# Layer 1's q product with a second Strassen step in four of its seven products

## The chip, the cores and the metric

The kernel runs on one core of a Trainium2 chip. The core has a matrix engine (TensorE: PE in the profile, PEld for its weight loads), a vector engine (DVE), a scalar engine (ACT), a general engine (POOL) and a queue engine (SP) that starts most transfers between HBM and the on-chip memory SBUF. PE writes its results to a second on-chip memory, PSUM, from which DVE and ACT take them. Every engine works through its own list of instructions in order, and waits for others through semaphores. The metric is the time of one execution in microseconds (us) on the device.

## The reference

Eight samples x of 512 channels by 1024 positions (32 x 32) go through two attention blocks, all in fp32. What matters here is the second one:

```python
def _L1_conv_ref(x, gn_gamma, gn_beta, wq, bq, wk, bk, wv, bv, wo, bo):
    mean = jnp.mean(x, axis=(1, 2, 3), keepdims=True)
    var = jnp.var(x, axis=(1, 2, 3), keepdims=True)
    n = (x - mean) * jax.lax.rsqrt(var + EPS)
    n = n * gn_gamma[None, :, None, None] + gn_beta[None, :, None, None]
    nf = n.reshape(b, c, h * w)
    q = jnp.einsum('oc,bcs->bos', wq, nf) + bq[None, :, None]
    k = jnp.einsum('oc,bcs->bos', wk, nf) + bk[None, :, None]
    v = jnp.einsum('oc,bcs->bos', wv, nf) + bv[None, :, None]
    attn = jax.nn.softmax(jnp.einsum('bci,bcj->bij', q, k) * c ** (-0.5), axis=-1)
    out = jnp.einsum('oc,bcs->bos', wo, jnp.einsum('bcj,bij->bci', v, attn)) + bo[None, :, None]
    return x + out.reshape(b, c, h, w)
```

The first block is a normalisation over groups of 16 channels, attention with eight heads of 64 channels, a projection, and `x + projection`. Its result is the x above.

## The kernel before

**Matrix products.** A product of 512 x 512 weights with 512 channels x 1024 positions is done by Strassen's method in Winograd's form: weights and data are cut into 2 x 2 quarters (`A11`.. and `B11`..), the sums `S1`..`S4` and `T1`..`T4` of them are formed, and seven products of quarters take the place of eight. A quarter of the data is `[128, 2, 512]`: two chunks k of 128 channels, 512 positions. A quarter product therefore takes two matmuls of 128 x 128 weights by 512 columns for each of two output chunks c. An fp32 matmul of the program is two PE instructions in the profile.

Products that run "twice" (q and k of layer 0, V of layer 1) apply the method a second time to four of the seven products, `PAIRS`: each of those four is again seven products, of 128 x 128 weights by half the columns. The three that remain are called lines (`A11 B11`, `S2 T2`, `S3 T3`) and add up in one PSUM bank for each output chunk. The quarter sums that the second step needs are made by `sums_a` from the weights (stored in HBM once, reloaded by `WeightTwice`) and by `quarters_b` from the data: three DVE instructions for each of `B21`, `T1`, `B22`, `T4`.

**Layer 1's weights.** Since q and k meet only in q'k, one matrix wqk1 takes the place of both; "q" is wqk1' x, and x itself stands for k. In the same way wvo1 is V and the output projection in one. Normalisation is not applied to x: `norm.c` is a bias of q worked out from mean and deviation, and `norm.factor` goes into the exponential.

**Order.** The program is unrolled over the eight samples, and the order on PE, DVE and ACT is the order in which the code is written (`manual_schedule`). A product is a Python generator that yields after each of its steps; `together` lets several take turns, and `at_steps` runs hooks after step n. What a hook issues stands in its engine's list at that place, so an early instruction that waits holds up all that stands behind it on its engine.

The stages of one sample that matter here, with the names of the code:

- `pairs_qk_twice` (layer 0, of the next sample): steps 0 to 13 are the second-step products of L862, steps 14 to 19 the lines of L869, added by DVE on L585. At hook 18 and 19 `divide_at` (L980) divides the attention's result by its sums, and `combine2` (L1030) makes T1 to T4 of the projection's data.
- `project` (PE on L632 into `ps_p`): `together(project(w, 0), project(w, 1))`, ten steps. ACT copies partial results (L425), DVE adds (L1229), adds the residual (L1215, x is complete there) and takes statistics of every chunk and half of x with `norm.of_half` (`bn_stats`, L318); `norm.of_channels` (`bn_aggr`, L321) brings them together at the end.
- `attention1`, `make_q` (PE on L632 into `ps_q`): the seven products of q, ten steps. At its hooks DVE makes T1 to T4 (`combine.make`, L400), the mean and deviation of the sample (`mean_of_all`, `deviation`: two small matmuls on L299 stand among q's), and the quarter sums for V (`halve_b`: L494 and L500). ACT finishes q with scale gamma and bias `norm.c` (L1291).
- `make_v_twice` (PE on L890 and L647): V's product, with the quarter sums of `halve_b`.
- scores, exponentials, values and the output follow.

At the start of the program the merged weights are made (`product`, `product_in_quarters`), their rows scaled by gamma on ACT (`scale_rows`, L235), the sums `S1`..`S4` formed (`finish`, L194) and the second-step sums made and stored (`WeightTwice(..., make)`, L477).

## Time and profile before

| | us |
|---|---|
| median of 3 runs | 2834.16 (2832.84 to 2834.77) |
| the profiled execution, its own time | 2834.0 |
| its span, from first to last instruction | 2832.3 |
| PE busy in the span | 2815.8 (mean granted TensorE clock 0.999) |
| sample 1: `project` on PE | 593.02 to 618.39: 25.37, DVE busy 17.81, ACT 3.51 |
| sample 1: q on PE | 618.39 to 642.87: 24.48, DVE busy 18.88, ACT 8.61 |
| longest wait of PE shown anywhere | 2.0 (before V's lines in the last sample) |

In the timeline a row is a run of equal instructions: its start in us from the start of the span, how long it took, the engine, the line, what is written and read, the shape, and how many there were; in brackets the idle time of that engine before it and what ended it. The start of a PE row is when it really began; its end is modelled, since matmuls are pipelined, so the distance from start to start is what counts. The same holds on DVE and ACT, where the next instruction starts some 0.1 us before the last one is written, unless it needs its result.

### The profile page before, as it was taken

Reading aid. Unit: us, or ns where it says so; the run is one execution under the profiler, and the core shown is the slowest. Engines: PE = TensorE matmul, PEld = TensorE weight load, DVE = VectorE, ACT = ScalarE, POOL = GpSimd, SP = SyncE. Lnnn points to the kernel's source line nnn. Section 1 sums busy time; section 2 is a strip of 40 time slices with the busy share of each in tenths; the row PEclk is TensorE's granted clock in tenths of the full one; section 3 lists DMA queues with packets and bytes.
Section 4 is the critical chain, followed back from the end, with each engine's and each line's share of the span. In section 5 each row is a group of like instructions: output and inputs, shape, how many; then the busy total and the mean of one; then the engine's idle time right before and its main releaser. Section 6 shows DMA issues by size and latency. Waiting matters only on the chain.

```text
span 2832.3 us, 38612 instructions
## 1 busy us (share of the span) xinstructions
PE 2815.8 (99%) x15496; PEld 1549.6 (55%) x15496; DVE 2124.0 (75%) x2979; ACT 1101.2 (39%) x1536; POOL 273.6 (10%) x236
## 2 busy tenths in 40 slices
PE   9999999999999999999999999999999999999999
PEld 5434765347643476444773456734567346673365
DVE  6677696767867778776777777777777777767877
ACT  3462324623256232552325522265232642326432
POOL 0000220003100040000400004000040000400011
PEclk9999999999999999999999999999999999999999
DMA  8422131321323213133131331313213142121001
GB/s 290 164 76 86 54 125 64 87 89 53 112 68 91 83 68 104 59 91 108 56 108 45 88 108 56 108 49 96 96 59 105 49 119 72 64 88 55 8 16 39
DMA packets 81123, 237.75 MB, mean 84 GB/s; under 512 B 21512, under 2 KB 22312, under 8 KB 74536
## 3 DMA queue, kind: packets, MB, share of 16 engines
q1 hardware_dynamic: 74456, 212.11, 23.1%
q10 hardware_dynamic: 6480, 23.10, 2.4%
q8 instruction: 124, 2.03, 0.3%
q14 instruction: 63, 0.52, 0.1%
HBM read 179.37 MB, written 31.98 MB: 75 GB/s over the span
## 4 chain that ended last, share of the span: by engine, by line
PE 89%; DVE 7%; DMA 2%; issue 1%; SPq 0%; ACT 0%; POOL 0%; DVEq 0%; POOLq 0%
PE s L941 16%; PE ps_o L960 15%; PE ps_q L632 8%; PE ps_v L647 7%; PE ps_o L1535 7%; PE ps_p L632 5%; PE ps_l L1371 4%; PE ps_s L1354 4%; PE ps_s_qk L862 4%; PE ps_l_qk L869 3%; PE ps_l_v L647 3%; PE ps_s L1371 3%; PE ps_o_qk L862 3%; PE ps_s_v L890 2%; PE ps_s_two L1665 2%; PE ps_o_v L890 1%
## 5 line engine op out<-in xcount | busy, mean ns | idle before, releaser
L798 ACT ACTIVATE p<-s 128x1024 f32<-128x1024 f32 x512 | 523.7, 1025 | 329.0 <-PE s L941 322.2
L800 DVE TENSOR_TENSOR acc<-acc,p 128x1024 f32<-128x1024 f32 x384 | 469.9, 1224 | 100.9 <-ACT p L798 92.5
L960 PE MATMUL ps_o<-p,v 64*64 64x512 f32 x4096 | 528.6, 589 | 0.0
L941 PE MATMUL s<-c_q,c_k 64*64 64x512 f32 x3584 | 465.1, 590 | 0.0
L960 PEld LDWEIGHTS ps_o<-p,v 64*64 64x64 f32 x4096 | 156.6, 133 | 282.9 <-issue 278.0
L941 PEld LDWEIGHTS s<-c_q,c_k 64*64 64x64 f32 x3584 | 134.7, 133 | 253.2 <-issue 236.1
L339 POOL TENSOR_TENSOR rstd<-rstd,minus_half 128x4 f32<-128x4 f32 (+1 forms) x16 | 19.8, 1239 | 2081.8 <-DVE rstd L338 2081.8
L1535 PE MATMUL ps_o<-t_p,s_v 128*128 128x512 f32 x384 | 168.2, 594 | 0.0
L800 DVE TENSOR_TENSOR acc<-p,p 128x1024 f32<-128x1024 f32 x64 | 78.3, 1224 | 80.0 <-ACT p L798 80.0
L1345 ACT ACTIVATE p<-p,factor 128x512 f32<-128x512 f32 (+1 forms) x112 | 85.3, 780 | 115.7 <-DVE p L1381 90.9
L1535 PEld LDWEIGHTS ps_o<-t_p,s_v 128*128 128x128 f32 x384 | 72.3, 190 | 91.3 <-issue 89.2
L1359 ACT COPY p<-ps_s 128x512 f32<-128x512 f32 x96 | 53.1, 588 | 177.0 <-PE ps_s L1354 177.0
L632 PE MATMUL ps_p<-t_p,w_p 128*128 128x512 f32 x256 | 115.2, 598 | 5.9 <-DVE u_p L1229 4.6
L1381 DVE TENSOR_TENSOR p<-ps_l,p 128x512 f32<-128x512 f32 x136 | 90.1, 684 | 40.5 <-PE ps_l L1371 40.2
L632 PE MATMUL ps_q<-t,w_wqk 128*128 128x512 f32 x256 | 116.1, 598 | 0.0
L425 ACT COPY u_v<-ps_v 128x512 f32<-128x512 f32 x48 | 28.1, 586 | 204.9 <-PE ps_v L647 195.8
L1381 DVE TENSOR_TENSOR p<-ps_s,p 128x512 f32<-128x512 f32 x112 | 74.9, 685 | 37.9 <-PE ps_s L1371 37.9
L647 PE MATMUL ps_v<-w_v,t_again 128*128 128x256 f32 x448 | 99.0, 379 | 0.0
L425 ACT COPY u_p<-ps_p 128x512 f32<-128x512 f32 x48 | 28.1, 585 | 174.1 <-PE ps_p L632 174.1
L425 ACT COPY u_q<-ps_q 128x512 f32<-128x512 f32 x54 | 31.2, 578 | 160.7 <-PE ps_q L632 160.7
L647 PEld LDWEIGHTS ps_v<-w_v,t_again 128*128 128x128 f32 x448 | 85.1, 190 | 11.6
L632 PEld LDWEIGHTS ps_p<-t_p,w_p 128*128 128x128 f32 x256 | 47.4, 190 | 72.4 <-issue 53.6
(463 smaller groups left out, 4948.2 us busy)
## 6 DMA issues: line engine op xcount, KB each, us to landing
x<-in_x SPq DMA_DIRECT2D x92, 512.0 KB, 6.5
w_qk<-stored_qk SPq DMA_DIRECT2D x14, 1792.0 KB, 7.1
w_wqk<-stored_wqk SPq DMA_DIRECT2D x8, 1792.0 KB, 7.6
fold<-acc SPq DMA_DIRECT2D x56, 256.0 KB, 3.1
inv<-inv_rows SPq DMA_DIRECT2D x56, 256.0 KB, 5.0
qk_twice<-stored_qk_twice ACTq DMA_DIRECT2D x28, 512.0 KB, 6.3
w_wvo<-stored_wvo SPq DMA_DIRECT2D x8, 1792.0 KB, 7.5
out<-x SPq DMA_DIRECT2D x28, 512.0 KB, 4.7
```

What stands on the lines that cost most here:

```text
L425: nc.scalar.copy(us[n][:, :width], line[:, :width])
L632: nc.tensor.matmul(bank, w[a][:, k, c * P : (c + 1) * P], bs[b][:, k, :], start=fresh and k == 0, stop=k == 1, skip_group_check=True,)
L647: nc.tensor.matmul(bank[:, u * 2 * P : (u + 1) * 2 * P], bs[b][:, k, n * P : (n + 1) * P], w[a][:, k, :], start=fresh and u == k == 0, sto ...
L798: nc.scalar.activation(p, s, AF.Exp, scale=factor)
L800: nc.vector.tensor_tensor(acc, first, p, ALU.add)
L862: nc.tensor.matmul(bank[:, i * 2 * P : (i + 1) * 2 * P], parts[a][x], twice_b[v][y], start=start and i == 0, stop=True, skip_group_check=True,
L941: nc.tensor.matmul(s[cols, j, :], ks[pair][k0 // HALF][rows, k0 % HALF : k0 % HALF + HD], qs[pair][g][rows, :], start=True, stop=True,)
L960: nc.tensor.matmul(o[cols, half, :], vs[kt][rows, c0 : c0 + HD], p[rows, j, :], start=kt == 0, stop=kt == NT - 1,)
L1354: nc.tensor.matmul(bank, bs[v][:, k, t * P : (t + 1) * P], q_parts[a][:, k, :], start=a == "A11" and k == 0, stop=k == 1, skip_group_check ...
L1371: nc.tensor.matmul(bank[:, u * 2 * P : (u + 1) * 2 * P], v[y][:, u * P : (u + 1) * P], a[x], start=start and u == 0, stop=True, skip_group ...
L1381: nc.vector.tensor_tensor(at(r, t), bank, at(r, t), ALU.add)
L1535: nc.tensor.matmul(bank, v_parts[kt // 2][a][:, kt % 2, c * P : (c + 1) * P], p_parts[kt // 2][b][:, kt % 2, cols], start=fresh and kt == ...
```

## The change

- q's product now runs "twice" as V's does, with its own order of pairs, `PAIRS_Q`. One generator makes both output chunks: two second-step products (f for `A12 B21` and `S4 B22`, s for `S1 T1` and `A22 T4`) around the lines. Its second-step weights are reloaded for each sample (`WeightTwice("wqk1")`: two transfers of 512 KB on ACT's queue), and made and stored once at the start.
- The quarter sums of x serve q and V. Those of `B21` and `B22` move into the stage before, `project`.
- Gamma of q's output channels is multiplied into the weights at the start (`scale_both`, on DVE, with a row of gamma loaded by one more transfer), so q needs only a bias at its end.
- The statistics of half of x are taken by ACT: for each chunk one half is taken by DVE (`first_half`), the other by two ACT instructions with accumulators (`second_half`), brought together by six small DVE instructions (`both_halves`).
- `combine2` of the projection's T2 to T4 moves from the hook ahead of `project` into its steps, and the four divisions change places.

```diff
+        def first_half(self, cc, half):
+            part = self.part[:, cc, 0, :]
+            nc.vector.bn_stats(part, piece(self.xs, cc, half))
+            nc.vector.bn_aggr(self.stat[:, :, cc], part)
+
+        def second_half(self, cc, half):
+            x = piece(self.xs, cc, half)
+            to = onepool.tile([P, HALF], FP, tag="held", name=f"from_0_{self.name}_{cc}")
+            nc.scalar.activation(to, x, AF.Identity, accum_out=self.part[:, cc, 1, 0:1])
+            to = onepool.tile([P, HALF], FP, tag="held", name=f"from_mean_{self.name}_{cc}")
+            nc.scalar.activation(
+                to, x, AF.Square, bias=self.stat[:, 0, cc : cc + 1], scale=-1.0,
+                accum_out=self.part[:, cc, 1, 1:2],
+            )
...
+    PAIRS_Q = [[("A12", "B21"), ("S4", "B22")], [("S1", "T1"), ("A22", "T4")]]
...
-                18: [lambda pair=pair: divide_at(pair, 0) for pair in couple],
-                19: [lambda pair=pair: divide_at(pair, 1) for pair in couple]
-                + [lambda n=n: combine2(n, 1) for n in range(1, 5)],
+                18: [lambda g=g: divide_at(couple[0], g) for g in range(2)],
+                19: [
+                    lambda: divide_at(couple[1], 0), lambda: combine2(1, 1),
+                    lambda: divide_at(couple[1], 1),
+                ],
...
-                    norm.of_half(chunk, half)
+                    if i == half:
+                        norm.first_half(chunk, half)
+                    else:
+                        norm.second_half(chunk, half)
+                    if (i, half, c) == (1, 0, 1):
+                        ready.halve("B21")
...
-        at_steps(together(project(w, 0), project(w, 1)), {})
-        for cc in range(NC):
-            norm.of_channels(cc)
+        hooks = {} if last else {2 * n - 3: [lambda n=n: combine2(n, 1)] for n in range(2, 5)}
+        hooks[0] = [ready.load]
+        hooks[7] = [lambda: ready.halve("B22")]
+        at_steps(together(project(w, 0), project(w, 1)), hooks)
...
+        def make_q(w):
...
+                for bank, x, y, start, use, r, t in [
+                    (line, "A11", "B11", True, nc.scalar.copy, 0, 0),
+                    (single, "A12", "B21", True, add, 0, 0),
+                    (line, "S2", "T2", False, nc.scalar.copy, 0, 1),
+                    (single, "S1", "T1", True, nc.scalar.copy, 1, 1),
+                    (line, "S3", "T3", False, add, 1, 1),
+                    (single, "S4", "B22", False, add, 0, 1),
+                    (line, "A22", "T4", False, nc.scalar.copy, 1, 0),
+                ]:
...
+            def take(r):
+                c11 = first[r][:, 0, :]
+                nc.vector.tensor_tensor(c11, lines[r], c11, ALU.add)
+
+            quarters = pair(PAIRS_Q[0], first, "f")
+            for n in range(2):
+                next(quarters)
+                yield
+            for r in range(2):
+                multiply(r, "A11", "B11", True)
+                yield
+            for n in range(5):
+                next(quarters)
+                if n == 0:
+                    take(0)
+                if n == 4:
+                    take(1)
+                yield
+            for r in range(2):
+                multiply(r, "S2", "T2", False)
+                c12 = first[r][:, 1, :]
+                nc.vector.tensor_tensor(c12, lines[r], c12, ALU.add)
+                yield
+            yield from pair(PAIRS_Q[1], second, "s")
+            for r in range(2):
+                nc.scalar.activation(
+                    piece(qs, r, 0), first[r][:, 0, :], AF.Identity, bias=norm.c[:, r : r + 1]
+                )
+                final(r, 0, 1, second[r][:, 0, :], first[r][:, 1, :])
+            for r in range(2):
+                multiply(r, "S3", "T3", False)
+                for n, half in enumerate([1, 0]):
+                    final(r, 1, half, lines[r], second[r][:, n, :])
+                yield
...
+        def statistics():
+            norm.both_halves()
+            norm.mean_of_all()
+
+        at_steps(make_q(w), {
+            1: [lambda: combine.make(1)],
+            6: [lambda: combine.make(2)],
+            8: [lambda: twice_w.append(WeightTwice("wvo1"))],
+            9: [lambda: combine.make(4)],
+            10: [lambda: ready.halve("T1"), lambda: ready.halve("T4")],
+            12: [statistics],
+            13: [lambda: combine.make(3)],
+            14: [norm.deviation],
+            16: [norm.untaken],
         })
...
-            wqk1.scale_rows(V_NW1)
+            wqk1.scale_both(V_NW1, gamma_row)
...
+                lambda: WeightTwice("qk02", both_of(w)), lambda: WeightTwice("wqk1", columns_of(wqk1)),
```

`final` is one DVE instruction (`x + norm.c + y`); `add` and `take` are one each; `nc.scalar.copy` is ACT. In `attention1` the old `make_q` and its hooks are removed.

More of the change, by code (lines that the diff above doesn't have):

```diff
@@ L79, in two_attention_blocks @@
     vectors: bass.AP,
+    gamma1: bass.AP,
     out: bass.AP,
@@ L235, in scale_rows, with scale_both @@
                     nc.scalar.activation(a, a, AF.Identity, scale=vec[:, by + cc : by + cc + 1])
+        def scale_both(self, by, row):
+            for cc in range(NC):
+                for to, a in self.moving(cc):
+                    nc.vector.scalar_tensor_tensor(
+                        a, a, vec[:, by + cc : by + cc + 1], row[:, to], ALU.mult, ALU.mult
+                    )
         def finish(self):
@@ L323, in of_channels, with both_halves @@
             )
+        def first_half(self, cc, half):
[11 more added lines that the diff above has]
+            )
+        def both_halves(self):
+            mean, var = self.stat[:, 0, :], self.stat[:, 1, :]
+            d, q = self.part[:, :, 1, 0], self.part[:, :, 1, 1]
+            nc.vector.scalar_tensor_tensor(d, d, 1.0 / HALF, mean, ALU.mult, ALU.subtract)
+            nc.vector.scalar_tensor_tensor(mean, d, 0.5, mean, ALU.mult, ALU.add)
+            nc.vector.scalar_tensor_tensor(q, q, 1.0 / HALF, var, ALU.mult, ALU.add)
+            nc.vector.scalar_tensor_tensor(d, d, -0.5, d, ALU.mult, ALU.mult)
+            nc.vector.tensor_tensor(var, q, d, ALU.add)
+            nc.vector.tensor_scalar(var, var, 0.5, None, ALU.mult)
         def mean_of_all(self):
@@ L1205, in layer0 @@
         bias = made["bias0"]
-        later = []
+        later, ready = [], Ready(xs, b)
         def project(w, c):
@@ L1247, in layer0, with __init__, load, halve @@
         w = next_weight().parts[0]
-        at_steps(together(project(w, 0), project(w, 1)), {})
-        for cc in range(NC):
-            norm.of_channels(cc)
+        hooks = {} if last else {2 * n - 3: [lambda n=n: combine2(n, 1)] for n in range(2, 5)}
+        hooks[0] = [ready.load]
+        hooks[7] = [lambda: ready.halve("B22")]
+        at_steps(together(project(w, 0), project(w, 1)), hooks)
         if last:
             held(invs.pop(end), f"inv_0_{b}_{end}_1")
-        return xs, norm, qs_next, ks_next
-    def attention1(xs, norm, b, at_values):
+        return xs, norm, ready, qs_next, ks_next
+    class Ready:
+        def __init__(self, xs, b):
+            self.combine, self.quarters, self.b = Combined(f"1_{b}"), {}, b
+            self.combine.take(xs)
+        def load(self):
+            self.weights = WeightTwice("wqk1")
+        def halve(self, name):
+            self.quarters[name] = quarters_b(
+                self.combine.parts[name], tile2(f"{name}_twice_{self.b}")
+            )
+    def attention1(xs, norm, ready, b, at_values):
         last = b + 1 == B
@@ L1266, in attention1 @@
         qs = quarters_of(f"q_1_{b}")
-        w = next_weight().parts[0]
+        w = next_weight()
         twice_w = []
-        combine, later = Combined(f"1_{b}"), []
-        combine.take(xs)
+        combine = ready.combine
         bs = combine.parts
-        twice_a, twice_b = {}, {}
+        twice_a, twice_b = {}, ready.quarters
         def halve_a(name, t=None, engine=nc.vector):
@@ L1278, in halve_a @@
             twice_a[name] = sums_a(q, flat(tile2(f"{name}_twice_{b}")) if t is None else t, engine)
-        def halve_b(name):
-            twice_b[name] = quarters_b(bs[name], tile2(f"{name}_twice_{b}"))
-        def make_q(c):
-            def done(i, half, bank, u):
-                n, to = c + 2 * i, piece(qs, c + 2 * i, half)
-                if u is not None:
-                    nc.vector.tensor_tensor(u, bank, u, ALU.add)
-                    bank = u
-                def scaled():
-                    nc.scalar.activation(
-                        to, bank, AF.Identity, bias=norm.c[:, n : n + 1],
-                        scale=vec[:, V_NW1 + n : V_NW1 + n + 1],
-                    )
-                if i == half == 0:
-                    later.append(scaled)
-                else:
-                    scaled()
-            return strassen(by_channels(w, c, bs), done, f"q_1_{b}_{c}")
@@ L1303, in attention1, with pair, add, multiply @@
-        at_steps(together(make_q(0), make_q(1)), {
-            0: [lambda: combine.make(1)],
-            1: [lambda: combine.make(2)],
-            2: [norm.mean_of_all, lambda: combine.make(3)],
-            3: [lambda: halve_b("B21")],
-            4: [norm.deviation, lambda: combine.make(4)],
-            6: [lambda: halve_b("T1")],
-            7: [lambda: halve_b("B22")],
-            8: [lambda: halve_b("T4")],
-            5: [lambda: twice_w.append(WeightTwice("wvo1")), norm.untaken, lambda: later.pop(0)(), lambda: later.pop(0)()],
+        def make_q(w):
+            parts = ready.weights.all(columns_of(w))
+            first, second = ([tile2(f"{n}_q_1_{b}_{r}") for r in range(2)] for n in ["c11", "c22"])
+            lines = [banks("o", f"ps_l{r}_q_1_{b}") for r in range(2)]
+            spares[:] = [line[:, 1, :] for line in lines]
+            lines = [line[:, 0, :] for line in lines]
+            def pair(products, to, name):
+                line, single = (banks("s", f"ps_{name}{n}_q_1_{b}")[:, 0, :] for n in range(2))
+                def add(at, bank):
+                    nc.vector.tensor_tensor(at, bank, at, ALU.add)
+                for bank, x, y, start, use, r, t in [
[7 more added lines that the diff above has]
+                ]:
+                    for i, (a, v) in enumerate(products):
+                        nc.tensor.matmul(
+                            bank[:, i * 2 * P : (i + 1) * 2 * P], parts[a][x], twice_b[v][y],
+                            start=start and i == 0, stop=True, skip_group_check=True,
+                        )
+                    use(
+                        to[r][:, :, t * 2 * P : (t + 1) * 2 * P],
+                        bank.rearrange("p (i q) -> p i q", i=2),
+                    )
+                    yield
+            def multiply(r, a, v, fresh):
+                by_channels(w.parts[0], r, bs)(lines[r], a, v, fresh)
+            def final(r, i, half, x, y):
+                n = r + 2 * i
+                nc.vector.scalar_tensor_tensor(
+                    piece(qs, n, half), x, norm.c[:, n : n + 1], y, ALU.add, ALU.add
+                )
+            def take(r):
[24 more added lines that the diff above has]
+                    piece(qs, r, 0), first[r][:, 0, :], AF.Identity, bias=norm.c[:, r : r + 1]
+                )
+                final(r, 0, 1, second[r][:, 0, :], first[r][:, 1, :])
[3 more added lines that the diff above has]
+                    final(r, 1, half, lines[r], second[r][:, n, :])
+                yield
+            spares.clear()
@@ L1724, in two_attention_blocks @@
         norm = norm0(xs_next, 0)
+        gamma_row = tile2("gamma_row")[:, 0, :]
+        nc.sync.dma_start(gamma_row, gamma1.to_broadcast([P, C]))
         class Through(Rows):
@@ L1778, in two_attention_blocks @@
             4: [lambda: combine.make(4)], 5: [lambda: WeightTwice("wvo1", columns_of(wvo1))],
-            7: [wqk1.finish], 8: [waiting[0].finish], 9: [lambda: WeightTwice("qk02", both_of(w))],
+            7: [wqk1.finish], 8: [waiting[0].finish], 9: [
+                lambda: WeightTwice("qk02", both_of(w)), lambda: WeightTwice("wqk1", columns_of(wqk1)),
+            ],
         })
@@ L1786, in two_attention_blocks @@
                 ahead = [norm0(load_x(b + 1, nc.sync), b + 1)]
-            xs, norm, qs, ks = layer0(bs, qs, ks, b, ahead[0] if b + 1 < B else None)
+            xs, norm, ready, qs, ks = layer0(bs, qs, ks, b, ahead[0] if b + 1 < B else None)
             at_values = {}
@@ L1802, in two_attention_blocks @@
                 bs = combine_next.parts
-            attention1(xs, norm, b, at_values)
+            attention1(xs, norm, ready, b, at_values)
 @with_exitstack
@@ L2180 @@
         "n_v1": np.ascontiguousarray(inputs["L1_conv_wv"]),
+        "gamma1": np.ascontiguousarray(np.asarray(inputs["L1_conv_gn_gamma"]).reshape(1, C)),
     }
```

## The prediction

> **What bounds the kernel now.** I read the page first: PE is busy for 99% of the span and makes 89% of the chain that ended last, so what counts is how many matmul columns PE streams and where it stands still.

> ```profile
> PE 2815.8 (99%) x15496; PEld 1549.6 (55%) x15496; DVE 2124.0 (75%) x2979; ACT 1101.2 (39%) x1536; POOL 273.6 (10%) x236
> PE 89%; DVE 7%; DMA 2%; issue 1%; SPq 0%; ACT 0%; POOL 0%; DVEq 0%; POOLq 0%
> ```

> Then PE's timeline in sample 1 (the others repeat it):

> ```profile
> 569.76 0.59 PE L862 MATMUL ps_s_qk<-t,w_qk 128*128 128x256 f32 x2
> 570.20 0.59 PE L862 MATMUL ps_s_qk<-x,w_qk 128*128 128x256 f32 x2
> ...
> 593.02 7.03 PE L632 MATMUL ps_p<-o,w_p 128*128 128x512 f32 x16
> 600.73 12.67 PE L632 MATMUL ps_p<-t_p,w_p 128*128 128x512 f32 x28 [0.68 <-DVE u_p L1229]
> ...
> 618.39 7.03 PE L632 MATMUL ps_q<-x,w_wqk 128*128 128x512 f32 x16
> 625.25 1.88 PE L632 MATMUL ps_q<-t,w_wqk 128*128 128x512 f32 x4
> 626.97 0.28 PE L299 MATMUL ps_q<-stat,in_sample 128*128 128x4 f32 x2
> ...
> 642.87 0.61 PE L890 MATMUL ps_s_v<-w_wvo,x 128*128 128x128 f32 x4
> ```

> Starts tell the pace: 16 instructions from 618.39 to 625.25 are 0.429 us each at 512 columns; two from 569.76 to 570.20 (0.4317 over the long run of these rows) are 0.216 each at 256. q takes 642.87 - 618.39 = 24.48. PE stands still only at the projection's start.

> Last, DVE and ACT, since q's new product leans on both:

> ```profile
> 612.14 0.69 DVE L318 BATCH_NORM_STATS2 part<-x 128x6 f32<-128x512 f32 x1
> 612.75 0.67 DVE L1229 TENSOR_TENSOR u_p<-ps_p,u_p 128x512 f32<-128x512 f32 x1
> 613.46 0.75 DVE L1215 SCALAR_TENSOR_TENSOR x<-u_p,bias,x 128x512 f32<-128x512 f32 x1
> 614.24 0.69 DVE L318 BATCH_NORM_STATS2 part<-x 128x6 f32<-128x512 f32 x1
> 614.85 0.73 DVE L1215 SCALAR_TENSOR_TENSOR x<-ps_p,bias,x 128x512 f32<-128x512 f32 x1
> ...
> 636.26 0.68 DVE L494 TENSOR_TENSOR T_twice<-t 128x512 f32<-128x512 f32 x1
> 636.98 0.88 DVE L500 TENSOR_TENSOR T_twice<-t,T_twice 128x256 f32<-128x256 f32 x2
> 637.78 0.68 DVE L1287 TENSOR_TENSOR u_q<-ps_q,u_q 128x512 f32<-128x512 f32 x1
> ```

> ```profile
> 2677.64 0.58 ACT L425 COPY u_p<-ps_p 128x512 f32<-128x512 f32 x1 [1.13 <-PE ps_p L632]
> 2678.13 0.63 ACT L808 ACTIVATE held_inv<-inv 128x512 f32<-128x512 f32 x1
> 2678.66 0.19 ACT L808 ACTIVATION_READ_ACCUMULATOR held_inv<-inv 128x1 f32 x1
> ```

> Start to start on DVE: 0.60 for a 512-wide sum, 0.72 if the next one needs it, 0.66 to 0.79 for a three-operand one, 1.13 for a 1024-wide one (L400), 1.52 for a set of quarter sums (636.26 to 637.78). DVE is busy 18.88 of q's 24.48 us, so little is free there. Other rows give the latencies: PE to ACT 0.20, PE to DVE 0.27, DVE or ACT to PE 0.06, and 0.10 lost when PE restarts.

> **PE's work.** Before, 56 instructions of 512 columns for each sample: 24.01. After, 56 of 256 and 24 of 512: 12.09 + 10.29 = 22.38. With the two small statistics matmuls (0.14 each) the stage would be 22.66 without waits. That is the gain: 1.6 a sample, 13 in all.

> **q's stage, step by step.** I lay the new lists against each other, t = 0 being q's first matmul (618.39). DVE's chain starts in the projection with the sum of chunk 2's second half, at t = -7.77 as now. Two chunks follow at 0.73 + 0.79 + 0.72 + 0.12 (the last two are the new `bn_aggr`'s, spaced as 23.26, 23.98 and 24.10 at the start of the program): to -3.05. B22's quarter sums, now ahead of the last x: to -1.53. Then x of chunk 2 half 0 (0.66), chunk 0 half 1 (0.71 + 0.66), chunk 3 half 0 (starts 0.50, written 1.23), B21's quarter sums (1.27 to 2.79), chunk 1 half 1: written at 4.25. Now q's f product wants chunk 3 at t = 0.86: PE waits 0.4 for it. Its lines run to 5.7.

> ACT takes statistics of chunk 1 half 1 from 4.29. The two accumulating instructions do not stand in the trace in this form. Bounds: 0.58 each, the spacing of L808 out of PSUM, and 0.85, an SBUF activation with pointer operands (L1291 takes 0.81) that waits for its neighbour; I take 1.46 for the pair, by the row 0.63 with its read. Only then, 5.75 to 6.34, does ACT copy f's first bank, for which PE (since 5.7) waits to 6.5, and DVE, idle since 4.16, waits to 6.37 with the `add` at the head of its queue; behind that stand T1, T2, T4 and all that follows.

> From there DVE: add 6.37, T1 6.97, take 8.18, add 9.36 (waits for PE), T2 9.96 to 11.18, add 11.09, take 11.89 (waits for ACT's copy of f's seventh), c12 13.33 (waits for PE's line), T4 13.93, c12 15.06, T1's quarter sums 15.66, T4's 17.18, s's first add 18.70, then `both_halves`: its mean, the second of six small instructions (0.25 apart, as the dependent ones at 632.95 and 633.20), is written at 19.77. PE meanwhile loses 0.4 at f's last step and S2 T2, does s's first two steps by 16.50, and there stands the small matmul of the mean (hook 12), in PE's own order: it waits until 19.8. That is 3.3 us, all of PE's queue behind it; s's third step would have waited for T4's quarter sums to 18.4 anyway. The rest: mean 20.07, s's remaining five steps with the deviation among them to 24.78, lines to 28.21. V follows at once, since its first banks are free by then and DVE is done with q at 30, before V's third step needs its second pair of banks (30.9).

> So q takes 28.2 in place of 24.48, 3.7 more for each sample: 5.5 of waits less the 1.6 of work and what was lost before. Eight samples: +29.8.

> **The projection's start.** Now PE loses 0.95 at 600.73 (16 instructions from 593.02 end at 599.88, plus the restart) and 0.38 two steps later, since four sums T1 to T4 stand on DVE ahead of L1229. With three of them gone later that goes. But couple[1]'s first division moves behind two bias additions (L585, 0.66 each): on DVE 592.83 and 593.43 for the first two divisions, 594.03 and 594.69 the additions, 595.35 the third, written 596.04, while PE wants it at 595.60: 0.6 lost. T2 to T4 are then made with 1 us and more to spare. Gain 0.73 in seven samples: -5.1. (The last sample keeps its own order.)

> **The start of the program.** `scale_both` puts eight 256-wide instructions on DVE (0.35 to 0.40 each, 3.0), `WeightTwice("wqk1")` sixteen sums (those of L477 take 3.73). Layer 0's first V sum (L681) starts on DVE at 65.79 now, and PE goes on to the next product at 67.13. 6.7 more on DVE, less the 2.5 that it was idle from 51.7 to 58.9 (0.81, 0.97, 0.74), puts it at 70.0 to 70.7 with its result: about 3.3 lost, once. Bounds 0 and 6.7. On SP's queue one transfer of gamma (256 KB) and two stores of 512 KB come in, each an issue of 0.33 to 0.5; behind the stores stand eight fetches of q's bias (8.68 to issue, done at 76.6 now), whose readers start at 85.89: hidden by some 7.

> **What is hidden.** The reload of wqk1's sums: issued near 595, two transfers of the kind that lands in 6.3, needed at 624.9; were the cover gone, up to 6 a sample. Its issue costs ACT 0.33 + 0.44, where ACT is idle 2.85. ACT's eight statistics (under 7 us a sample) but for the last pair, whose price is above. V's reload, now issued near 631, needed 650. The saved scaling on ACT is worth nothing. The extra 8 MB are 3.5% of the 237.75 MB that are moved, at a mean of 84 GB/s against the 290 that the first slice shows.

> [...]

> **Sum.** 29.8 - 5.1 + 3.3 = +28; the profiled execution took 2834.0 (its span 2832.3 and 1.7 around), like the median 2834.16. So 2862.

> **Rivals.** (1) DVE keeps up. One mechanism: if the mean is ready when s's second step ends, PE's wait at hook 12 is gone, and if ACT's copy is not late either, q takes some 23 and the sum is 8 x (-1.5) - 5.1 + 3.3: 2820. For it: DVE has 5.6 idle in q's stage now. Against: sixteen sums in q where six were, and two waits of DVE for ACT and PE that I can name. The break-even is where q takes 24.7, that is 3.5 less waiting a sample than I count. (2) Only the long wait is mis-sized: DVE's waits shorter by 1 to 2 us a sample (ACT's pair at 1.16 gives 0.3 of it, PE then stopped by T4's quarter sums alone gives another 1.4): 2846 to 2854. (3) ACT runs late for all four pairs, at 2 us a pair: its last pair ends at 7.3 in place of 5.75, all that follows is 1.5 later, 2874.

> **How the numbers follow.** My sum 0.60, rival 2 0.18, rival 3 0.13, rival 1 0.09. 2862 is the likeliest's. 0.2% of the time is 5.7 us, about what a measurement of this kernel can tell. Range 2846 to 2875: its own bounds (startup 0 to 6.7, ACT's pair +-2.4 in all, 0.5 a sample for DVE's spacings, 4 in all) with rivals 2 and 3; rival 1 is left out. Rival 1 splits into faster 0.07 and within 0.2% 0.02; slower 0.91.

> **What would show it.** In the profile after: q's stage on PE 28 long, with a wait of 3 us on PE at the statistics' matmul released by DVE's `both_halves`, DVE idle 2 us before the first `add` and released by ACT; the wait at 600.73 gone and one of 0.6 on the division's result. Wrong it would be if q's stage takes 23 to 25, or PE's wait sits on a transfer.

## The result and the profile after

The changed kernel takes 2881.76 us (median; 2880.92 to 2881.89), the kernel before 2834.47 beside it: 1.0167 times as long, 95% interval 1.0154 to 1.0179. The forecast was 2862, from 2846 to 2875. The profiled execution has a span of 2880.0, that of before 2832.3: 47.7 more, where the sum had 28.

The page's first rows, busy times and the shares of the chain that ended last:

```profile
PE 2831.6 (98%) x15688; PEld 1593.4 (55%) x15688; DVE 2171.1 (75%) x3099; ACT 1119.8 (39%) x1624; POOL 266.4 (9%) x236
PE 86%; DVE 12%; issue 1%; ACT 1%; DMA 0%; POOL 0%; DVEq 0%; ACTq 0%; POOLq 0%
```

PE has less to stream than before and is yet shown busy for 15.8 us longer. A busy time can only grow like that if instructions took longer. DVE's share of the chain has gone from 7% to 12%.

Sample 1 in the timeline (start, length, engine, line; in brackets the idle time before and what ended it):

```profile
603.72 2.74 PE L668 MATMUL ps_p<-o,w_p 128*128 128x512 f32 x6
606.79 4.56 PE L668 MATMUL ps_p<-o,w_p 128*128 128x512 f32 x10 [0.33 <-DVE o L1016]
...
628.35 1.03 PE L1363 MATMUL ps_f_q<-x,w_wqk 128*128 128x256 f32 x4
...
634.73 0.69 DVE L1351 TENSOR_TENSOR c_q<-ps_f_q,c_q 128x512 f32<-128x512 f32 x1 [2.16 <-ACT c_q L1367]
634.75 2.94 PE L1363 MATMUL ps_f_q<-B_twice,wqk_twice 128*128 128x256 f32 x12 [0.60 <-ACT c_q L1367]
...
643.21 1.93 PE L1363 MATMUL ps_s_q<-t,w_wqk 128*128 128x256 f32 x8
...
648.08 0.59 PE L307 MATMUL ps_l_q<-stat,in_sample 128*128 128x4 f32 x2 [2.95 <-DVE stat L354]
648.53 3.76 PE L1363 MATMUL ps_s_q<-T_twice,wqk_twice 128*128 128x256 f32 x8
652.08 0.43 PE L307 MATMUL ps_l_q<-spread,in_sample 128*128 128x4 f32 x2
...
659.68 0.61 PE L926 MATMUL ps_s_v<-w_wvo,x 128*128 128x128 f32 x4
```

With t = 0 at 628.35, DVE's first sum stands at t = 6.38 (forecast 6.37) and the mean's matmul starts at 19.73 (19.8): the schedule held. But q takes 659.68 - 628.35 = 31.33 (28.2), and the surplus lies behind the long wait. The eight 256-column instructions from 648.53 to 652.08 are 0.44 us apart; those from 643.21 were 0.22. Same width, same kind of operands, twice the time.

Where PE stood still (what waits, for what, us in all, times, longest):

```profile
PE ps_l_q L307 <- DVE stat L354: 23.7, 8, 3.0
PE ps_f_q L1363 <- ACT c_q L1367: 5.6, 8, 1.4
PE ps_v L683 <- DVE v L717: 3.9, 1, 3.9
```

The wait for the mean is the same 3 us in all eight samples. Its aftermath is not: six us from the end of that wait in each of the eight samples, with the granted clock (PEclk, before the DMA share):

```profile
297.28:303.28 6.00, 6.00 (x27) 4.67 (x28) 4.96 (x18) 1.84 (x4) 0.55 (x1) 1.00 0.00 0
648.08:654.08 6.00, 6.00 (x16) 5.01 (x17) 2.65 (x11) 1.17 (x2) 0.55 (x1) 0.50 0.00 0
1001.67:1007.67 6.00, 6.00 (x21) 4.80 (x22) 3.36 (x13) 1.17 (x2) 0.55 (x1) 0.72 0.01 3
1354.15:1360.15 6.00, 6.00 (x21) 4.82 (x22) 3.46 (x13) 1.17 (x2) 0.56 (x1) 0.72 0.00 0
1706.64:1712.64 6.00, 6.00 (x16) 5.01 (x17) 2.65 (x11) 1.17 (x2) 0.55 (x1) 0.50 0.00 0
2060.11:2066.11 6.00, 6.00 (x21) 4.78 (x22) 3.36 (x13) 1.17 (x2) 0.56 (x1) 0.72 0.01 3
2412.66:2418.66 6.00, 6.00 (x16) 5.01 (x17) 2.66 (x11) 1.17 (x2) 0.55 (x1) 0.50 0.00 0
2748.21:2754.21 6.00, 6.00 (x27) 4.66 (x28) 4.97 (x18) 1.84 (x4) 0.55 (x1) 1.00 0.01 3
```

Samples 0 and 7 keep full speed and stream 27 instructions; 1, 4 and 6 run at half speed throughout (16 instructions), the others for part of it. q takes 28.29, 31.32, 29.96, 29.97, 31.20, 29.96, 31.42 and 29.04 us in samples 0 to 7. In sample 0, with the clock whole, it takes what was forecast.

The stretches in which the trace's clock records grant one half:

```
start (us)   length (ns)
  70.81        6827        (program's start, behind the wait for L717)
 647.66        6827
1002.64        3413
1354.22        3413
1705.79        6827
2060.78        3413
2412.35        6827
```

They last 3413 ns or twice that, and their starts lie apart by whole multiples of 3413.33 ns: (1002.64 - 647.66) / 3.41333 = 104.0, and from each start to the next it is 169, 104, 103, 103, 104 and 103 of them. So in this trace the half-speed stretches lie on one grid of windows of 3413.33 ns, and the wait of 3 us falls on it differently in each sample.

The account, from the two profiles (us, after less before):

| | forecast | measured |
|---|---|---|
| first projection begins later | +3.3 | +7.57 (252.92 for 245.35) |
| projection, samples 0 to 6 | -5.1 | -4.98 |
| projection, sample 7 | 0 | +0.35 |
| q at full clock (as in the run fill3) | +29.8 | +31.2 |
| half-speed stretches in q | 0 | +14.1 |
| all else | 0 | -0.5 |
| sum | +28 | +47.7 |

The first row can be taken apart on PE. These are the second half of layer 0's first V product and the product that follows it, before the change:

```profile
67.13 12.25 PE L647 MATMUL ps_v<-w_v,t 128*128 128x256 f32 x56
...
84.40 3.60 PE L632 MATMUL ps_q<-x,w_qk 128*128 128x512 f32 x8
```

and after it:

```profile
71.67 15.28 PE L683 MATMUL ps_v<-w_v,t 128*128 128x256 f32 x56 [3.90 <-DVE v L717]
...
91.97 3.60 PE L668 MATMUL ps_q<-x,w_qk 128*128 128x512 f32 x8
```

The later sum on DVE (L717) makes PE go on 4.54 later. From there to the next product PE takes 20.30 in place of 17.27, since the half-speed stretch from 70.81 lies in between: 3.03 more. So 14.1 + 3.0 = 17.1 of the 19.7 us that the sum missed are half speed.

### The profile page after: what moved, and what is told of

It reads as the page before. It is cut to its first block, busy times and chain, and to the rows that moved or that the text cites. A ratio compares the mean times of both kernels' runs of the same rounds, so it can differ in the third digit from the quotient of the medians.

```text
span 2880.0 us, 39302 instructions
## 1 busy us (share of the span) xinstructions
PE 2831.6 (98%) x15688; PEld 1593.4 (55%) x15688; DVE 2171.1 (75%) x3099; ACT 1119.8 (39%) x1624; POOL 266.4 (9%) x236
## 3 DMA queue, kind: packets, MB, share of 16 engines
q1 hardware_dynamic: 74888, 213.42, 22.7%
## 4 chain that ended last, share of the span: by engine, by line
PE 86%; DVE 12%; issue 1%; ACT 1%; DMA 0%; POOL 0%; DVEq 0%; ACTq 0%; POOLq 0%
PE s L977 15%; PE ps_o L996 15%; PE ps_o L1654 7%; PE ps_v L683 7%; PE ps_l_qk L905 5%; PE ps_l L1490 4%; PE ps_s L1473 4%; PE ps_p L668 4%; PE ps_s_qk L898 3%; PE ps_l_v L683 3%; PE ps_s L1490 3%; PE ps_o_qk L898 3%; PE ps_s_v L926 2%; PE ps_s_q L1363 2%; PE ps_s_two L1784 2%; PE ps_l_q L668 2%
## 5 line engine op out<-in xcount | busy, mean ns | idle before, releaser
L834 ACT ACTIVATE p<-s 128x1024 f32<-128x1024 f32 x512 | 523.4, 1024 | 329.3 <-PE s L977 321.0
L374 POOL TENSOR_TENSOR rstd<-rstd,minus_half 128x4 f32<-128x4 f32 (+1 forms) x16 | 12.6, 788 | 2172.6 <-DVE rstd L373 2172.6
L668 PE MATMUL ps_p<-o,w_p 128*128 128x512 f32 x192 | 88.6, 597 | 2.3 <-DVE o L1016 2.3
L683 PE MATMUL ps_v<-w_v,x 128*128 128x256 f32 x384 | 86.8, 379 | 0.0
```

What stands on the lines that cost most here:

```text
L668: nc.tensor.matmul(bank, w[a][:, k, c * P : (c + 1) * P], bs[b][:, k, :], start=fresh and k == 0, stop=k == 1, skip_group_check=True,)
L683: nc.tensor.matmul(bank[:, u * 2 * P : (u + 1) * 2 * P], bs[b][:, k, n * P : (n + 1) * P], w[a][:, k, :], start=fresh and u == k == 0, sto ...
L834: nc.scalar.activation(p, s, AF.Exp, scale=factor)
```

## The experiments

The first four ask what made the rows behind the wait slow, and what the wait is made of. "Before" is 2834.45 us beside them.

**fill3 and fill1.** PE gets something to do while it waits:

```diff
         def statistics():
             norm.both_halves()
+            for _ in range(3):      # fill1: range(1)
+                nc.tensor.matmul(
+                    spares[1], w.parts[0]["A11"][:, 0, :P], bs["B11"][:, 0, :],
+                    start=True, stop=True, skip_group_check=True,
+                )
             norm.mean_of_all()
```

> The changed kernel with three more matmuls of 512 columns (six instructions of 0.43 us, into an unused bank that nobody reads) ahead of the statistics' small matmul on PE, in the time in which PE waits for the mean. My theory: the 2.95 us of waiting halve PE's clock in the window that follows; with 0.4 us of waiting left, the half-speed stretches in the samples go (the one at the program's start stays), every sample's q takes the 28.3 us that sample 0 shows, and the time is 2881.8 less some 14: 2867 (2864 to 2870). Rival: the rows after the wait are slow for another reason (their operands, DVE's accesses, the reload of weights): they keep 0.43 us in place of 0.216, and the time stays at 2881 to 2883.

2865.8 us (ratio 1.0112, 1.0095 to 1.0129): 16 us faster for more work. PE in sample 1 of fill3 (timeline):

```profile
641.93 1.93 PE L1363 MATMUL ps_s_q<-t,w_wqk 128*128 128x256 f32 x8
643.69 2.74 PE L1421 MATMUL ps_l_q<-x,w_wqk 128*128 128x512 f32 x6
646.80 0.39 PE L307 MATMUL ps_l_q<-stat,in_sample 128*128 128x4 f32 x2 [0.37 <-DVE stat L354]
647.04 1.97 PE L1363 MATMUL ps_s_q<-T_twice,wqk_twice 128*128 128x256 f32 x8
```

L1421 is the filling. The mean's matmul comes at the same t = 19.7 after q's start (627.09), so the filling costs nothing, and the rows from 647.04 run at 0.23 each. q takes 28.27 to 28.29 in samples 0 to 5, 28.38 and 29.03 in the last two; no half-speed stretch is left in a sample. With the wait filled, the mean granted clock is 0.999 (0.993 in the changed kernel) and the rows behind it take 0.23 us each in place of 0.44: that the rows had been slow because of the clock, and the clock because PE had stood still, is shown here.

> The same with one such matmul (two instructions, 0.86 us): a wait of 2.1 us is left. All half-speed stretches of the changed kernel begin on a grid of 3413 ns, and each follows a grid window with at least 0.61 of it idle, while windows with 0.51 idle are followed by none. If the clock goes by that share, 2.1 us (0.61 of a window at most, and most often cut by a window's edge) halve it in no sample or one or two: 2867 to 2871. If it goes by any wait of over 2 us, six or more samples keep their stretch: 2878 to 2882.

2871.27 us (1.0131, 1.0114 to 1.0148). The wait left is 2.09 us in seven samples and 2.19 in sample 6 by the bracket, 2.25 by starts in sample 7; q takes 29.96, 29.95 and 30.56 in samples 3, 5 and 7, which have a stretch, and 28.27 to 28.37 in the others. Three where I expected two at most; but neither all nor none, as a rule by the wait's length alone would have it.

**act_later and stat14.** The first puts ACT's last two statistics instructions behind f's first copy, the second asks for the mean two steps later:

```diff
                     if i == half:
                         norm.first_half(chunk, half)
+                    elif (i, half, c) == (0, 1, 1):
+                        ready.rest = lambda: norm.second_half(chunk, half)
                     else:
                         norm.second_half(chunk, half)
...
+            0: [ready.rest],
```

```diff
-            12: [statistics],
             13: [lambda: combine.make(3)],
-            14: [norm.deviation],
-            16: [norm.untaken],
+            14: [statistics],
+            16: [norm.deviation],
+            17: [norm.untaken],
```

> The changed kernel with ACT's two statistics instructions of the last half of x behind ACT's copy of f's first bank. By the schedule: the 2.16 us for which DVE waits before its first sum go, and PE's 0.6 at the same place; but DVE's next sums wait for PE's products, so only some 0.8 of it reaches the mean, PE's wait for the mean stays near 2.9 us, and the half-speed stretches stay in most samples: 2881.8 less 8 x 0.8 = 2875 (2870 to 2880). Rival: the whole 2.16 us reach the mean, its wait shrinks to 1.6 us, the stretches go: 2881.8 - 8 x 2.16 - 14 = 2850.

2870.11 us (1.0125, 1.0108 to 1.0142). q at full clock takes 27.41 (samples 2 and 7), 0.88 less. PE's timeline in sample 1:

```profile
644.05 1.93 PE L1365 MATMUL ps_s_q<-t,w_wqk 128*128 128x256 f32 x8
648.92 0.39 PE L307 MATMUL ps_l_q<-stat,in_sample 128*128 128x4 f32 x2 [2.95 <-DVE stat L354]
649.16 2.46 PE L1365 MATMUL ps_s_q<-T_twice,wqk_twice 128*128 128x256 f32 x8
```

The wait is the same 2.95: PE and the mean moved by the same amount. So DVE's 2.16 of idle time before its first sum was not the cause of the long wait, since DVE would have stood for PE's next product instead. Six samples still lose part of their clock, but only sample 0 has a double stretch: the stretches cost 11.4 in place of 14.1, and q at full clock gives 7.8 in all in place of the 6.4 expected. That is most of the 5 us by which the time lies below the centre of what I expected.

> The changed kernel with the statistics two steps of PE later (hooks 14, 16 and 17 in place of 12, 14 and 16, and T3 ahead of them on DVE). By the schedule the mean comes at t = 20.4 in place of 19.8, but PE has two steps more to do before it: it stands 2.0 us for T4's quarter sums at s's third step and 0.2 for the mean. q takes 26.9 in place of 28.3, and a wait of 2.0 us (0.59 of a grid window of 3413 ns at most) halves the clock seldom: 2881.8 - 14 - 8 x 1.4 = 2856 (2853 to 2866). If the long wait is all the mean's own, however late it is asked for, the time stays above 2865.

2861.36 us (1.0094, 1.0078 to 1.0111), inside the expectation. q takes 27.46 (26.9 expected), except sample 7 with 28.22, where ACT is late, and sample 6 with 28.73, whose PE rows are:

```profile
2391.34 1.93 PE L1363 MATMUL ps_s_q<-t,w_wqk 128*128 128x256 f32 x8
2393.45 0.67 PE L1363 MATMUL ps_s_q<-T_twice,wqk_twice 128*128 128x256 f32 x2 [0.19 <-DVE T_twice L535]
2394.88 0.70 PE L1363 MATMUL ps_s_q<-T_twice,wqk_twice 128*128 128x256 f32 x2 [0.76 <-DVE T_twice L535]
2396.04 1.72 PE L1363 MATMUL ps_s_q<-T_twice,wqk_twice 128*128 128x256 f32 x4 [0.46 <-DVE c_q L1351]
```

No wait here is over 0.8 by its bracket, yet the clock halves at 2396.44. The bracket counts from the modelled end of a matmul. By starts and pace (the last instruction of the first row starts at 2392.88 and ends 0.216 later) PE is idle 0.35 us before the second row, 1.00 before the third and 0.73 before the fourth, and 0.10 inside the fourth: 2.18 us, all of it in the window from 2393.02 to 2396.44, or 0.64 of it. Behind that window the rows run at half speed (four from 2397.89 to 2399.74, 0.46 each, where those of the first row are 0.22 apart), though the longest single wait in it is 1.00.

The profiles of both kernels can be counted in the same way: PE's idle time by starts and pace in each window at full speed, leaving out the end of the program. In the changed kernel the seven windows that half speed follows were idle for 0.674 (the one from 1702.38) to 0.938 of their length, and of the others the idlest, from 292.67 in sample 0, for 0.572 (with the modelled ends, 0.615 and 0.514). In the kernel before, the idlest was idle for 0.575 (from 2723.30), with full speed behind it. Neither profile has a window between 0.575 and 0.674. The two statistics matmuls of 4 columns, counted by their columns or as the 0.11 us from one start to the next, change neither 0.572 nor 0.674.

The next four take parts of the change apart or put DVE's list in another order. Before: 2834.29.

**start_pool.** The sixteen sums at the start go to POOL (`WeightTwice` takes the engine as one more argument):

```diff
-    ... lambda: WeightTwice("wqk1", columns_of(wqk1)),
+    ... lambda: WeightTwice("wqk1", columns_of(wqk1), nc.gpsimd),
```

> The changed kernel with the sixteen sums of q's weights at the program's start (the second-step sums that are made once) on POOL in place of DVE. My theory: they are what layer 0's first V product waits 3.9 us for, and the half-speed stretch behind that wait costs 1.7 to 3.4 more: 2881.8 less 5.6 to 7.3 = 2875 (2872 to 2879, since the shift also moves the samples' waits on the clock's grid). POOL is idle there; its own sums of this size take 0.73 to 1.34 us, 14 to 17 in all, and their readers come 170 us later. Rival: something else at the start costs the 7.6 us by which the first projection is late (the stores, gamma's transfer, the scaling): 2880 to 2883.

2881.21 us (1.0157, 1.0141 to 1.0172): nothing gained, as my rival had it, but not for its reason. The first projection begins at 248.65 in place of 252.92 (the wait at V's first product is 1.48 in place of 3.9, with no half-speed stretch behind it). The 4.3 us are then lost again, 3.3 of them in q: with everything shifted, all eight samples have a stretch (twelve windows with one in V, nine before). Its four times run from 2873.48 to 2883.31, and the granted clock goes with them: 0.996 in the fastest, 0.993 in the other three. 0.003 of the span is 8.6 us, so this spread is the clock's as well; in which windows it was lost is known only for the one run that was profiled. The changed kernel's own four times, all at 0.993, lie within 1 us.

**early and early_start.** DVE's list in the order in which the operands come (with act_later's edit), then with start_pool's as well:

```diff
-            1: [lambda: combine.make(1)],
-            6: [lambda: combine.make(2)],
+            0: [ready.rest],
+            1: [lambda: combine.make(1), lambda: combine.make(2)],
+            4: [lambda: combine.make(4)],
+            7: [lambda: ready.halve("T1")],
             8: [lambda: twice_w.append(WeightTwice("wvo1"))],
-            9: [lambda: combine.make(4)],
-            10: [lambda: ready.halve("T1"), lambda: ready.halve("T4")],
-            12: [statistics],
-            13: [lambda: combine.make(3)],
-            14: [norm.deviation],
-            16: [norm.untaken],
+            9: [lambda: ready.halve("T4")],
+            13: [statistics],
+            14: [lambda: combine.make(3)],
+            15: [norm.deviation],
+            17: [norm.untaken],
```

> The changed kernel with DVE's list in q put in the order in which its operands come: ACT's last two statistics instructions behind f's first copy, T2 beside T1 (hook 1), T4 at hook 4, T1's quarter sums at 7, T4's at 9, the statistics at 13, T3 at 14, the rest at 15 and 17. By the schedule DVE then fills the time in which it waited, and the mean is written at t = 16.4 in place of 19.8, some 0.5 us after PE wants it. q takes 24.0 in place of 28.3, no half-speed stretch is left in a sample: 2881.8 - 14 - 8 x 4.3 = 2833 (2830 to 2842). Rival: DVE's work itself is too much for q's stage, in any order: q stays over 26 and the time over 2850.

2841.69 us (1.0025, 1.0015 to 1.0035): 40 us faster than the changed kernel, at the far end of what I expected. No stretch in any sample; q takes 24.97 (25.74 in sample 7), not 24.0. Sample 1's timeline names the rest:

```profile
632.99 1.21 DVE L435 TENSOR_TENSOR t<-x,t 128x1024 f32<-128x1024 f32 x1
...
634.86 1.13 PE L1365 MATMUL ps_f_q<-B_twice,w_wqk 128*128 128x256 f32 x4 [0.63 <-DVE c_q L1353]
...
642.41 0.39 PE L307 MATMUL ps_l_q<-stat,in_sample 128*128 128x4 f32 x2 [0.18 <-DVE stat L354]
```

T4 now stands on DVE ahead of a sum that PE needs, and the long wait for the mean is 0.18.

> Both edits together. 2833 less the wait of 3.9 us at the start and its half-speed stretch of 1.7 to 3.4: 2826 to 2828, which would be 7 us or 0.25% below the kernel before. By the rival of the run before, over 2845.

2837.66 us (1.0012, 1.0003 to 1.0021): not below the kernel before. It misses by q's 8 us and because the start gave 4.4 in place of 5.6 to 7.3: 1.5 of the wait of 3.9 is left.

**proj_only.** The kernel before with the projection's new order, and nothing else of the change:

```diff
-                18: [lambda pair=pair: divide_at(pair, 0) for pair in couple],
-                19: [lambda pair=pair: divide_at(pair, 1) for pair in couple]
-                + [lambda n=n: combine2(n, 1) for n in range(1, 5)],
+                18: [lambda g=g: divide_at(couple[0], g) for g in range(2)],
+                19: [
+                    lambda: divide_at(couple[1], 0), lambda: combine2(1, 1),
+                    lambda: divide_at(couple[1], 1),
+                ],
...
-        at_steps(together(project(w, 0), project(w, 1)), {})
+        hooks = {} if last else {2 * n - 3: [lambda n=n: combine2(n, 1)] for n in range(2, 5)}
+        at_steps(together(project(w, 0), project(w, 1)), hooks)
```

> The kernel before with one part of the change alone: the projection's divisions in their new order and the sums T2 to T4 in its steps. The stage took 25.31, 25.37, 25.12, 25.52, 25.54, 25.14 and 25.39 us in samples 0 to 6 and takes 24.63 after the change: 2834.4 less 4.98 = 2829.5. If the gain was owed to the rest of the change (V's and q's sums elsewhere), the time stays at 2834.

2830.65 us (0.9987, 0.9978 to 0.9996), the fastest of all, though 3.6 us below the kernel before and not 5.0. The stage takes 24.63 in samples 0 to 6, as after the change. That part's gain is its own.

**best1, best2, best3.** Three attempts at a version below both. best1 starts from early_start, moves f's lines ahead of its second step, T4 and T1's quarter sums behind the two sums, the statistics to hook 14, and the scaling at the start to ACT and POOL:

```diff
             next(quarters)
             yield
             for r in range(2):
                 multiply(r, "A11", "B11", True)
                 yield
+            next(quarters)
+            yield
...
+            2: [lambda: combine.make(1)],
+            3: [lambda: combine.make(2)],
+            7: [lambda: combine.make(4), lambda: ready.halve("T1")],
...
```

> early_start with what its trace still shows of waits in q: f's lines ahead of its second step (it stood 0.36 us for x), T4 behind the two sums after it (0.79 us of PE's wait for the first of these), the statistics one step later (0.43 us), and the scaling at the start on ACT and POOL in place of DVE (the first projection begins 3.06 us later than in the kernel before). q should take 23.2 to 23.6 us in place of 24.97 (22.66 would be without waits) and the first projection begin at 245.5: 2837.7 - 8 x 1.6 - 3 = 2822 (2819 to 2826), below both kernels and below the projection's new order alone (2830.7). Rival: the waits only move to the next operand in DVE's list, q stays at 24.5 or more: 2830 to 2835, and the second Strassen step of q is worth nothing in any order.

2853.75 us (1.0070, 1.0057 to 1.0084), worse than what it started from; q takes 27.12. PE in sample 1:

```profile
626.34 1.99 PE L667 MATMUL ps_l_q<-x,w_wqk 128*128 128x512 f32 x4 [0.73 <-DVE u_p L1273]
...
637.02 1.99 PE L667 MATMUL ps_l_q<-t,w_wqk 128*128 128x512 f32 x4 [1.28 <-DVE c_q L1385]
```

The edits made other operands late: the second line's bank is still held by the projection's last sum on DVE, the `take` that frees it for S2 T2 now stands behind T4 and a set of quarter sums, and the last lines wait 0.7 for a sum of the statistics. The start gained nothing either: the first projection begins at 248.59 (early_start: 248.41), and while POOL multiplies by gamma, sums of 128 columns on DVE take up to 0.81 us in place of 0.28.

best2 keeps PE's order, starts from early_start and moves less:

```diff
                     if (i, half, c) == (1, 0, 1):
+                        ready.halve("B22")
                         ready.halve("B21")
...
-        hooks[7] = [lambda: ready.halve("B22")]
...
-            4: [lambda: combine.make(4)],
-            7: [lambda: ready.halve("T1")],
-            8: [lambda: twice_w.append(WeightTwice("wvo1"))],
+            6: [lambda: combine.make(4)],
+            8: [lambda: twice_w.append(WeightTwice("wvo1")), lambda: ready.halve("T1")],
             9: [lambda: ready.halve("T4")],
-            13: [statistics],
-            14: [lambda: combine.make(3)],
+            14: [statistics, lambda: combine.make(3)],
             15: [norm.deviation],
...
```

> early_start with three moves in DVE's list and one on PE: B22's quarter sums behind the last x that f's second step needs (PE stood 0.36 us for it), T4 behind the first of the two sums and T1's quarter sums behind f's end (PE stood 0.79 for that sum), T4's quarter sums then end at t = 15.3, and the statistics go one step later (0.43) with T3 behind them. By the schedule q takes 23.4 in place of 24.97: 2837.7 - 8 x 1.5 = 2826 (2822 to 2831), below the kernel before and, by 4 us, below the projection's new order alone. Rival, as the run before it showed: each move makes another operand late, q stays at 24.7 or more: 2835 or above.

2833.66 us, 0.9999 of the kernel before (0.9990 to 1.0008). q takes 24.51 in all eight samples, where the old q takes 24.48. The matmul work saved is 1.6 us a sample, and waits take just that back: by starts PE is idle 1.9 us in sample 1's q, where it was idle 0.25 before the change. The only waits of PE that its list names in this stage are for DVE (0.4 a sample), and DVE is busy for 22.68 of the 24.51 us. That DVE is the bound is likely by this, not shown.

best3 puts T3 and T4 on POOL, which is idle there.

```diff
-        def make(self, n):
+        def make(self, n, engine=nc.vector):
...
-            nc.vector.tensor_tensor(p[f"T{n}"], x, y, ALU.subtract)
+            engine.tensor_tensor(p[f"T{n}"], x, y, ALU.subtract)
...
+                lambda: combine.make(3, nc.gpsimd), lambda: combine.make(4, nc.gpsimd),
...
```

> The kernel of the run before (2833.7, q 24.51) with T3 and T4 on POOL, which stands idle in q's stage, in place of DVE (two sums of 1024 columns, 1.13 to 1.22 us each on DVE), T1's quarter sums in two pieces where DVE waits, the rest in the same order. My theory: DVE's work is what bounds q by now (busy but for about 1 us between t = 4 and 21.5); with 2.4 us less of it PE waits only for single sums, q takes 23.2 to 23.6, and the time is 2833.7 - 8 x 1.1 = 2825 (2821 to 2829), faster than the kernel before by 0.3%. POOL's sums of 512 columns take 1.27 us alone and 1.71 beside others' accesses, so T4 ends between 2.6 and 3.4 us after T3 and is wanted 5 us after T2. Rival: DVE's instructions get longer while POOL works, or T4 comes too late: q at 24.5 or above, 2833 or more.

2837.79 us (1.0012, 1.0003 to 1.0021); q takes 25.03. DVE and POOL in sample 1:

```profile
624.49 0.68 DVE L1353 TENSOR_TENSOR c_q<-ps_f_q,c_q 128x512 f32<-128x512 f32 x1
624.79 2.36 POOL L435 TENSOR_TENSOR t<-x,x 128x1024 f32<-128x1024 f32 x1 [169.21 <-DVE x L1253]
625.09 3.14 DVE L435 TENSOR_TENSOR t<-x,x 128x1024 f32<-128x1024 f32 x1
628.26 1.23 DVE L435 TENSOR_TENSOR t<-x,t 128x1024 f32<-128x1024 f32 x1
...
629.62 2.35 POOL L435 TENSOR_TENSOR t<-x,t 128x1024 f32<-128x1024 f32 x1 [2.48 <-DVE t L435]
630.01 1.28 DVE L1353 TENSOR_TENSOR c_q<-ps_f_q,c_q 128x512 f32<-128x512 f32 x2
631.20 1.32 DVE L529 TENSOR_TENSOR T_twice<-t 128x512 f32<-128x512 f32 x1
```

DVE's T1 takes 3.14 where it takes 1.22 in best2's profile: POOL's sum ends at 627.15, and T1 at 628.23, 1.1 later, as if it had stood until POOL was done. The quarter sum at 631.20 takes 1.32 for 0.68 beside POOL's second sum, which ends at 631.97. The two sums from 630.01, which take one operand from PSUM, ran beside POOL at their usual 0.64. POOL took two sums of 1.22 off DVE's list, and two others of DVE's took 1.9 and 0.6 longer beside POOL's: about as much. The rival won, and so the run does not tell what less work on DVE would bring.

**no_gamma.** early_start with the scaling on ACT, as in the kernel before; it leaves the multiplication by gamma out:

```diff
-            wqk1.scale_both(V_NW1, gamma_row)
+            wqk1.scale_rows(V_NW1)
```

> early_start with the weights scaled by ACT as in the kernel before, and the multiplication by gamma left out (so q comes without gamma). It tells what the scaling on DVE costs at the start: with the sums on POOL the first projection still begins at 248.4 against 245.35 in the kernel before. If the eight scaling instructions on DVE (0.35 to 0.40 us each, 3.0 in all) are the rest, it begins at 245.4 and the time is 2837.7 - 3 = 2834.7. Rival: POOL's sums hold up DVE, as they did in the run before this one, or the two stores on SP's queue come ahead of what layer 0 waits for: it stays at 248, the time at 2837 to 2838.

2835.21 us (1.0005, 0.9995 to 1.0015). The first projection begins at 246.29 in place of 248.41: the scaling on DVE costs 2.1 at the start. For the last 0.9 against 245.35 the trace has a candidate, sums on DVE that last longer while POOL's run:

```profile
63.14 0.51 POOL L512 TENSOR_TENSOR wqk_twice<-wqk_twice,w_wqk 128x128 f32<-128x128 f32 x1
63.26 0.54 DVE L512 TENSOR_TENSOR qk_twice<-w_qk 128x128 f32<-128x128 f32 x1
```

The sixteen sums of `qk_twice` ahead of V's first take 4.66 us on DVE (62.57 to 67.23), 3.73 in the kernel before (62.06 to 65.79); those beside no sum of POOL's take 0.28 or 0.29 as before. So the run's rival came true in part. The two stores and gamma's transfer were not tried apart.

## Why the prediction was wrong, point by point

- **PE's work**: right. The timeline has the sum's 56 instructions of 256 columns and 24 of 512 in q, at its paces where the clock is whole.
- **q's stage**: right, to a tenth. 28.2 forecast, 28.29 in sample 0 and 28.27 to 28.38 in fill3's first seven. Sample 7, where ACT is later (PE waits 1.4 for it, not 0.6), takes 0.75 more; I had put all eight alike.
- **The clock: this step failed.** The sum and the range have every row behind a wait at full speed. Behind a wait of 2.95, six of eight samples ran at half speed for a window or two, 14.1 us in all (in samples 0 and 7 the grid cut the wait so that no window was idle for more than 0.57 of its length). The stretch behind the start's wait cost 3.0 more. The wait is about as long in all eight samples; what differed is how much of it fell into one window. If a share of 0.572 to 0.674 of a window (1.95 to 2.30 us) is the least that half speed follows, a wait of 3.11 us (by starts) puts that much into one window from 0.77 to 0.56 of the positions it can have, as an estimate from these numbers: (3.41 - 3.11 + 2 x (3.11 - 1.95)) / 3.41 = 0.77, and 0.56 with 2.30. Of 8 samples that is 4.5 to 6.1. With the 14.1 us added, the range's upper end would have been 2889, above the 2881.76 measured.
- **The projection**: right, -4.98 for -5.1, and proj_only shows the gain alone.
- **The start**: too small a term, 7.6 for 3.3, over the upper bound of 6.7 too. DVE's later sum holds PE up by 4.5 for the 3.3 forecast, inside the bounds. The other 3.0 are the half-speed stretch behind that wait, which the sum put at nothing: the same failed step as in q. With the sums on POOL 4.3 of the 7.6 go, the stretch among them, and with the scaling off DVE 2.1 more.
- **What is hidden**: PE's list of waits names no transfer; the reloads cost nothing that I could find.
- **The rivals**: (1) asked for less waiting; only a reordered list came near it, and best2 then ties with the kernel before. (2) named T4's quarter sums as the next stop behind the mean; stat14 shows them there. (3) needed ACT's last pair to end at t = 7.3; ACT's copy behind it began at 5.78, the 5.75 of the sum.

## What to carry to other kernels

Price a wait of PE by the idle time it puts into one clock window, together with other waits nearby, and not by its length alone: in the changed kernel windows idle for 2.30 us and more were followed by 3.41 or 6.83 us at half speed and those idle for 1.95 us and less were not, so a wait of 2.95 us cost q 1.7 to 3 more in six of eight samples. If PE must wait, matmuls that nobody reads brought 2881.76 to 2865.8 here (fill3), and asking for the late result two steps later brought it to 2861.36 (stat14). And before a product is made cheaper on PE, count what its sums add to the engine beside it: here, with that engine busy for 22.7 of 24.5 us, waits took back all that the product saved, even in the best order tried.
